# Attention batches turned by VectorE and through memory, and another order of transfers for the turned weights

## The chip, the core and the metric

The kernel runs on one core of a Trainium2 chip. The metric is the device time of one execution in microseconds (us); a kernel's time is the median of its runs. The core has a matrix engine (TensorE, PE in the profile; its weight loads are listed as PEld), a vector engine (VectorE, DVE), a scalar engine (ScalarE, ACT), a general engine (GpSimd, POOL) and SyncE (SP), which computes nothing here and issues nearly all transfers (DMAs). Sixteen DMA engines carry these out. Work happens in on-chip memory of 128 partitions; matmuls write to eight banks of an accumulation memory, each 128 x 512 numbers of float32.

## The reference

The input x has 16 batches of 512 tokens of width 256, all in float32. The block is a "macaron": half a feed-forward part, attention, half a feed-forward part again, with the same feed-forward weights both times.

```python
x = x + 0.5 * _L0_ffn_ref(_layernorm(x), ...)
x = x + _L0_attn_ref(_layernorm(x), Wq, bq, Wkv, bkv, Wo, bo)
x = x + 0.5 * _L0_ffn_ref(_layernorm(x), ...)
```

The feed-forward part is a mixture of 16 slots and 16 experts. The change lies in the attention alone: 16 heads of width 64, queries and keys rotated by position, causal softmax:

```python
q = rope(heads(x @ Wq + bq)); k, v = split(x @ Wkv + bkv); k = rope(heads(k))
scores = einsum('bhqd,bhkd->bhqk', q, k) / sqrt(64)      # masked above the diagonal
out = einsum('bhqk,bhkd->bhqd', softmax(scores), v)
return out @ Wo + bo
```

## The kernel before

All 16 batches stay on chip, with tokens along the partitions (four tiles of 128 tokens). First comes a feed-forward part (to about 430 us), then the attention (to about 1920 us), then the second feed-forward part.

The attention is a loop over 64 units, a unit being one batch and one group of four heads (`units`, L848). It is a pipeline written out by hand (L1101 to L1174): one pass of the loop, called a step here, works on up to four units at once. Step u makes the rotated queries and keys of unit u + 3 (`Rotated`, L886), the scores and exponentials of unit u + 2 (`Weights.scores`, L948; `exps`, L962), scales and turns the weights of unit u + 1 and computes its values (L920), and multiplies the turned weights of unit u with the values (`sums`, L1045) and with Wo (`leave`, L1065). Every engine and every queue takes its instructions in the order in which this loop writes them; the matmuls of a step stand in the order `p_av` (sums), `p_as` (scores of the last token tile), `p_v`, `p_q`, `p_k`, `p_v`, `p_as` (the other tiles), `p_ay` (Wo).

Two things are turned (tokens and another axis exchanged) in this loop.

The first is each batch, once in four units. Queries, keys and values need the normalized batch with its width along the partitions. `enter` (L866) normalizes it with ScalarE into two tiles `h`; `width` (L878) turns it with eight TensorE transposes of 128 x 128 (L883) into two accumulation banks, which ScalarE copies to the tile `ahT` (L884). For the first batch this is done ahead of the loop; for the others in the step in which u + 3 is the first unit of the batch (`fresh`, L1105), the same step whose queries and keys need it. In that step GpSimd also adds the output bias to the batch (`with_bias`, L874). The inverse deviations for a pair of batches come from `spread` (L852, ScalarE) and `scales` (L859, VectorE), one step apart, and from `token_stats` (L193, VectorE), spread over earlier steps.

The second is the softmax weights, in every step. VectorE turns blocks of 32 by 32 (`turn`, L989, instruction at L1001) from the tiles `pr` into the tile `sq`; this exchanges rows and columns within each block, but leaves each block in its group of 32 partitions. `move` (L1018) then brings the blocks to their groups: sixteen transfers, one for each pair of groups (q from, k to), 160 KB each, from `sq` to `prT`. Before the change a source row is one piece of 4 x 320 x 4 = 5120 bytes, and so is a destination row. The transfers run over k outside and q inside. Each of `sq` and `prT` exists once, so a step's turn waits until the transfers of the step before have read `sq`, and the sums (L1054) wait until they have landed.

SyncE issues these sixteen transfers as soon as VectorE has ended the turn, and in the step after a batch's last unit two stores of the finished batch (L1078). The feed-forward parts move their own turned weights through memory in a like way (`Squares`, L518): a store of 512 KB to memory (`leave`, L534) and four loads of 128 KB back (`onto`, L538).

Of the kernel before, what the change touches and what calls it, by code (L numbers as in the profile page):

```python
# [9 lines left out]
F32 = mybir.dt.float32  # L10
# [5 lines left out]
P = 128  # L16
NB, S, D = 16, 512, 256
NT = S // P
NC = D // P
GB = 4  # L20
PB = 2
# [13 lines left out]
HG = 4  # L35
NHG = AH // HG
SQ = 32
NSQ = P // SQ
# [9 lines left out]
def macaron_kernel(ctx: ExitStack, tc: tile.TileContext, a: dict, out: bass.AP):  # L48
# [795 lines left out]
    def attention(qp, wq, wk, wv, wo, cos, sin, row):  # L844
# [2 lines left out]
        ap = None  # L847
        units = [(b, hg) for b in range(NB) for hg in range(NHG)]  # L848
        nu = len(units)
        hTs, hs, qs, ks, vs, oTs, prTs, stds = {}, {}, {}, {}, {}, {}, {}, {}  # L850

        def spread(g):  # L852

            n = PB * NT
            std = small.tile([P, n], F32, tag="std8", name=f"std_g{g}")
            nc.scalar.activation(std, mvs[g][:, :, 1], AF.Sqrt, bias=eps)
            return std

        def scales(g, std):  # L859

            n = PB * NT
            rstds[g] = small.tile([P, n], F32, tag=f"rstd{g}", name=f"rstd{g}", bufs=1)
            nc.vector.reciprocal(rstds[g], std)
            pair_shift(g)

        def enter(b):  # L866

            hs[b] = [qp.tile([P, 2, D], F32, tag=f"rope{2 + k}", name=f"h{b}_{k}") for k in range(2)]
            for t in range(NT):
                i = (b % PB) * NT + t  # L870
                nc.scalar.activation(hs[b][t // 2][:, t % 2, :], xs[b][:, t, :], AF.Identity,
                                     bias=shifts[b // PB][:, i:i + 1], scale=rstds[b // PB][:, i:i + 1])

        def with_bias(b):  # L874
            for t in range(NT):
                nc.gpsimd.tensor_tensor(xs[b][:, t, :], xs[b][:, t, :], row, ALU.add)

        def width(b):  # L878
            hTs[b] = qp.tile([P, NC, S], F32, tag="hT", name=f"ahT{b}", bufs=2)
            for c in range(NC):  # L880
                pt = ps(f"p_ahT{b}_{c}")
                for t in range(NT):
                    nc.tensor.transpose(pt[:, t * P:(t + 1) * P], hs[b][t // 2][:, t % 2, c * P:(c + 1) * P], ident)  # L883
                nc.scalar.copy(hTs[b][:, c, :], pt)  # L884

        class Rotated:  # L886

# [2 lines left out]
            def __init__(self, u, nm, w, r):  # L890
                self.b, self.hg = units[u]
                self.nm, self.w, self.r, self.m = nm, w, r, {}
# [39 lines left out]
        class Weights:  # L932
# [56 lines left out]
            def turn(self, which, heads, of, src, dst):  # L989

                if heads[0] == 0 and which == 0 and len(of) == 2:
                    self.sq = ap.tile([P, NSQ, HG, blocks * SQ], F32, tag="sq", name=f"sq{self.nm}")
                pr = self.pr[which]

                def view(x, at, dims):
                    return bass.AP(x.tensor, x.offset + at, [list(x.ap[0])] + [[s, n] for s, n in dims if n > 1])
                j, nh = heads
                step = (7, 3)[which] * P  # L1000
                nc.vector.transpose(  # L1001
                    view(self.sq, j * blocks * SQ + dst[0] * SQ,
                         [(blocks * SQ, nh)] + [(s * SQ, n) for s, (_, n) in zip(dst[1:], of)]
                         + [(HG * blocks * SQ, NSQ), (1, SQ)]),
                    view(pr, j * step + src * P,
                         [(step, nh)] + [(s * P, n) for s, n in of] + [(SQ, NSQ), (1, SQ)]))

# [10 lines left out]
            def move(self):  # L1018


                prT = prTs[self.u] = ap.tile([P, NSQ, HG, blocks * SQ], F32, tag="prT", name=f"prT{self.nm}")
                for k in range(NSQ):
                    for q in range(NSQ):
                        nc.sync.dma_start(prT[k * SQ:(k + 1) * SQ, q, :, :], self.sq[q * SQ:(q + 1) * SQ, k, :, :])

            def turn_at_once(self):

# [37 lines left out]
        def leave(u, t0):  # L1065
            b, hg = units[u]
            py = ps(f"p_ay{b}_{hg}_{t0}")
            for t in range(2):
                for pair in range(HG // 2):
                    nc.tensor.matmul(py[:, t * D:(t + 1) * D], oTs[u][:, pair, (t0 + t) * P:(t0 + t + 1) * P],  # L1070
                                     wo[:, hg * (HG // 2) + pair, :],
                                     start=(pair == 0), stop=(pair == HG // 2 - 1))

            def added():
                xt = xs[b][:, t0:t0 + 2, :]
                nc.vector.tensor_tensor(xt, py.rearrange("p (t d) -> p t d", t=2), xt, ALU.add)
                if hg == NHG - 1:
                    nc.sync.dma_start(xout[b][:, t0:t0 + 2, :], xt)  # L1078
            return added
# [15 lines left out]
        ap = yield [lambda: width(0)] + queries_keys(0)  # L1095
        ws = {}
        seen = 2 * NHG
        with tc.manual_schedule(engines={mybir.EngineType.DVE, mybir.EngineType.Activation,
                                         mybir.EngineType.Pool, mybir.EngineType.SP}):
            gone = []  # L1100
            for u in range(-2, nu):  # L1101
                new = ws[u + 2] = Weights(u + 2) if u + 2 < nu else None
                qk = queries_keys(u + 3)
                old = ws.get(u + 1)
                fresh = u + 3 < nu and units[u + 3][1] == 0  # L1105
                if fresh:
                    enter(units[u + 3][0])
                if u + 2 == nu:
                    old.scaled((1, 0))
                    values(u + 1, 0)  # L1110
                    values(u + 1, 2)
                if u >= 0:
                    sums(u, 0)
                    sums(u, 1)
                if old and u + 2 == nu:
                    old.turn_at_once()
                elif old:
                    old.turn_most(0)
                    old.scaled((1, 0), slice(0, HG // 2))
                    old.turn_most(1)  # L1120
                    old.scaled((1, 0), slice(HG // 2, HG))
                    old.turn_most(2)
                    old.turn_most(3)
                    old.turn_corner()
                    old.turn_rest()
                    old.move()
                for one in gone:
                    one()
                if fresh:
                    with_bias(units[u + 3][0])  # L1130
                if u + 4 in stds:
                    scales((u + 4) // (PB * NHG), stds.pop(u + 4))
                if fresh:
                    width(units[u + 3][0])
                if new:
                    new.scores((3,))
                    new.exps((3,))

                for at in range(seen, min(u + 13, NB * NHG)):
                    token_stats(*divmod(at, NHG))  # L1140
                seen = max(seen, u + 13)
                if u >= NHG + 1:
                    token_stats(*divmod(u - NHG - 1, NHG))
                if new:
                    new.scaled((3,))
                if 0 <= u + 1 < nu - 1:
                    values(u + 1, 0)
                for one in qk:
                    one()
                if 0 <= u + 1 < nu - 1:  # L1150
                    values(u + 1, 2)
                if 0 <= u + 5 < nu and (u + 5) % (PB * NHG) == 0:
                    stds[u + 5] = spread((u + 5) // (PB * NHG))
                if new:
                    new.scores((2,))
                    new.scores((1, 0))
                    new.exps((2,))
                    new.exps((1, 0), lambda: new.scaled((2,)))

                if u == nu - NHG:  # L1160
                    for g in range(NB // PB - 1):
                        pair_rstd(g)
                if u == nu - 1:
                    for g in range(PB):
                        entered[g] = xs[g]
                        for t in range(NT):
                            i = (g % PB) * NT + t
                            nc.vector.tensor_scalar(xs[g][:, t, :], xs[g][:, t, :], mvs[g // PB][:, i, 0:1],
                                                    rstds[g // PB][:, i:i + 1], ALU.subtract, ALU.mult)
                gone = [leave(u, 0), leave(u, 2)] if u >= 0 else []  # L1170
                if u >= nu - 2:
                    for one in gone:
                        one()
                    gone = []  # L1174
            token_stats(NB - 2, NT - 1)
# [55 lines left out]
```

## Time and profile before

| What | us |
|---|---|
| median of 3 runs (2329.22 to 2330.73) | 2330.49 |
| the profiled execution, its own time | 2332.58 |
| its span in the trace | 2330.9 |
| L883, eight transposes of a batch: time that they hold TensorE in a step | 1.02 |
| L884, one of two evictions of a turned batch, mean | 0.588 |
| L1001, one block turn of 128 x 512, 128 x 768, 128 x 1024, mean | 0.669, 0.950, 1.202 |
| L1024, sixteen transfers of turned weights: issue on SyncE | 10.6 |

How to read it: the profile is one execution. Its span is the time from the first to the last instruction; the execution's own time is 1.7 us longer. Engine names are as above; "SPq" is SyncE's queue of transfers, L12 is line 12 of the kernel. A group's line gives the busy time, the mean length of one instruction and the idle time before it with what ended it. The DMA share is the mean busy share of the 16 DMA engines.

### The profile page before, as it was taken

What the parts mean: (1) busy time and instruction counts of PE and PEld (TensorE: products, weight loads), DVE (VectorE), ACT (ScalarE), POOL (GpSimd) and SP (SyncE); (2) the same over time, 40 slices, a digit from 0 to 9 for tenths busy, and PEclk for the clock granted to TensorE, in tenths of its full rate; (3) what the DMA queues carried; (4) which work ended last, traced back from release to release, by engine and by line L of the source; (5) the groups of instructions that cost most, each with busy time, mean ns of one, the idle gap of its engine ahead of it and who ended that gap; (6) DMA issues with size and microseconds to landing.
All of it is one profiled execution on the core that took longest, in us unless ns stands there. A gap on an engine that the chain in (4) does not pass through costs nothing. (4 is left out here: it accounts for less than half of the span.)

```text
span 2330.9 us, 42260 instructions
## 1 busy us (share of the span) xinstructions
PE 2285.0 (98%) x14496; PEld 1453.5 (62%) x14496; DVE 1754.1 (75%) x4658; ACT 1123.7 (48%) x3046; POOL 1061.9 (46%) x1692
## 2 busy tenths in 40 slices
PE   7999999999999999999999999999999999999999
PEld 5665588465656565565656565655656566664588
DVE  6742397888888888898888888888888874442387
ACT  4743243455455545554645545554555454542233
POOL 2210054565555565655656555556565541210043
PEclk9999999999999999999999999999999999999999
DMA  6839851345555464645455555546464543839834
GB/s 223 252 124 406 321 137 46 85 97 129 107 119 126 103 134 93 142 103 129 107 123 113 126 111 116 129 100 137 91 140 105 127 110 96 241 115 405 329 115 140
DMA packets 159710, 346.77 MB, mean 149 GB/s; under 512 B 38980, under 2 KB 98952, under 8 KB 151304
## 3 DMA queue, kind: packets, MB, share of 16 engines
q1 hardware_dynamic: 158636, 343.27, 55.4%
q8 instruction: 115, 1.88, 0.4%
q14 instruction: 99, 0.81, 0.1%
q10 hardware_dynamic: 860, 0.81, 0.1%
HBM read 148.95 MB, written 29.88 MB: 77 GB/s over the span
## 5 line engine op out<-in xcount | busy, mean ns | idle before, releaser
L986 POOL TENSOR_SCALAR pr<-pr,ars 128x512 f32<-128x512 f32 (+3 forms) x1024 | 522.1, 532 | 631.5 <-DVE ars L983 631.5
L978 ACT ACTIVATE pr<-pr,amn 128x512 f32<-128x512 f32 (+3 forms) x1024 | 560.5, 549 | 268.4 <-DVE amn L974 268.2
L974 DVE CUSTOM_DVE_ANT_0 pr<-p_as,causal 128x512 f32<-128x512 f32 (+3 forms) x1024 | 433.9, 484 | 96.6 <-PE p_as L956 96.6
L1001 DVE STREAM_TRANSPOSE sq<-pr 128x768 f32<-128x768 f32 x441 | 379.0, 906 | 0.2 <-issue 0.2
L956 PE MATMUL p_as<-k,q 32*128 32x128 f32 (+3 forms) x4096 | 325.3, 445 | 7.1 <-DVE k L904 3.4
L1054 PE MATMUL p_av<-prT,v 128*64 128x512 f32 (+3 forms) x2048 | 292.1, 438 | 1.9 <-DVE amn L974 1.9
L956 PEld LDWEIGHTS p_as<-k,q 32*128 32x128 f32 x4096 | 192.4, 186 | 107.4 <-issue 49.6
L920 PEld LDWEIGHTS p_v<-wv,ahT 128*128 128x128 f32 x1024 | 189.4, 190 | 97.4 <-issue 75.6
L920 PE MATMUL p_v<-wv,ahT 128*128 128x256 f32 x1024 | 248.1, 385 | 0.0
L923 ACT COPY v<-p_v 128x512 f32<-128x512 f32 x128 | 73.3, 574 | 353.1 <-PE p_v L920 353.1
L1070 PE MATMUL p_ay<-wo,aoT 128*128 128x256 f32 x1024 | 240.5, 388 | 0.2 <-ACT aoT L1061 0.2
L1054 PEld LDWEIGHTS p_av<-prT,v 128*64 128x64 f32 x2048 | 138.1, 138 | 161.7 <-issue 136.5
L898 PE MATMUL p_k<-ahT,wk 128*128 128x512 f32 x512 | 230.6, 592 | 0.4 <-DVE amn L974 0.4
L898 PE MATMUL p_q<-ahT,wq 128*128 128x512 f32 x512 | 230.5, 593 | 0.2 <-ACT ahT L884 0.2
L1070 PEld LDWEIGHTS p_ay<-wo,aoT 128*128 128x128 f32 x1024 | 190.8, 191 | 32.0 <-ACT aoT L1061 0.6
L978 ACT ACTIVATION_READ_ACCUMULATOR pr<-pr,amn 128x1 f32 x1024 | 191.7, 187 | 0.0
L898 PEld LDWEIGHTS p_k<-ahT,wk 128*128 128x128 f32 x512 | 97.2, 190 | 122.7 <-issue 110.5
L898 PEld LDWEIGHTS p_q<-ahT,wq 128*128 128x128 f32 x512 | 97.1, 190 | 95.8 <-issue 85.4
L717 POOL TENSOR_TENSOR kbd<-kT,own 128x256 f32<-128x256 f32 x32 | 19.7, 619 | 267.4 <-DVE kT L680 235.5
L1061 ACT ACTIVATE aoT<-p_av,bcol 128x512 f32<-128x512 f32 x128 | 87.4, 684 | 108.9 <-PE p_av L1054 108.9
L770 PE MATMUL p_cy<-vw,catT 128*128 128x256 f32 x512 | 120.8, 379 | 0.0
L548 PE MATMUL p_ds<-hT,qk 128*128 128x512 f32 x256 | 118.3, 606 | 2.3 <-ACT hT L241 2.3
(167 smaller groups left out, 3252.0 us busy)
## 6 DMA issues: line engine op xcount, KB each, us to landing
prT<-sq SPq DMA_DIRECT2D x1008, 160.0 KB
w<-in_e_W_dram SPq DMA_DIRECT2D x64, 1024.0 KB
w<-in_e_Wg_dram SPq DMA_DIRECT2D x32, 1024.0 KB
out_dram<-x SPq DMA_DIRECT2D x64, 256.0 KB
awaya<-sqa SPq DMA_DIRECT2D x25, 512.0 KB
atT<-awaya SPq DMA_DIRECT2D x100, 128.0 KB
xl<-in_attn_x_dram SPq DMA_DIRECT2D x16, 512.0 KB
xl<-out_dram SPq DMA_DIRECT2D x16, 512.0 KB
```

The costliest lines, as they stand in the source:

```text
L548: nc.tensor.matmul(psc, qk[:, k, c * P:(c + 1) * P], hT[:, k, :], start=(k == 0), stop=(k == NC - 1))
L770: nc.tensor.matmul(py[:, t * D:(t + 1) * D], atT[:, c, t * P:(t + 1) * P], vws[b][:, c, :], start=(c == 0), stop=(c == NC - 1))
L898: nc.tensor.matmul(pq, self.w[:, k, at:at + P], hTs[self.b][:, k, :], start=(k == 0), stop=(k == NC - 1))
L920: nc.tensor.matmul(pv[:, t * 256:(t + 1) * 256], hTs[b][:, k, (t0 + t) * P:(t0 + t + 1) * P], wv[:, k, hg * HG * DQ:(hg + 1) * HG * DQ], s ...
L956: nc.tensor.matmul(banks[j][:, at:at + w], q[n][j * 32:(j + 1) * 32, i * P:(i + 1) * P], k[n][j * 32:(j + 1) * 32, :w], start=(n == 0), st ...
L974: nc.vector.tensor_tensor_reduce(out=self.at(i, j), in0=banks[j][:, at:at + w], in1=causal[:, S - w:], scale=-1.0 / math.sqrt(DQ), scalar= ...
L978: nc.scalar.activation(self.at(i, j), self.at(i, j), AF.Exp, bias=self.mn[:, i, j:j + 1], scale=-1.0, accum_out=self.rs[:, i, j:j + 1])
L986: nc.gpsimd.tensor_scalar(self.at(i, j), self.at(i, j), self.rs[:, i, j:j + 1], 1.0, ALU.mult, ALU.mult)
L1001: nc.vector.transpose(view(self.sq, j * blocks * SQ + dst[0] * SQ, [(blocks * SQ, nh)] + [(s * SQ, n) for s, (_, n) in zip(dst[1:], of)] + ...
L1054: nc.tensor.matmul(po[j * DQ:(j + 1) * DQ, :].rearrange("d (a f) -> d a f", a=NSQ)[:, :, t * SQ:], vs[u][:, t, head * DQ:(head + 1) * DQ], ...
L1061: nc.scalar.activation(oTs[u][:, pair, :].rearrange("d (i a y) -> d a i y", i=NT, a=NSQ), po.rearrange("d (a i y) -> d a i y", i=NT, a=NSQ ...
L1070: nc.tensor.matmul(py[:, t * D:(t + 1) * D], oTs[u][:, pair, (t0 + t) * P:(t0 + t + 1) * P], wo[:, hg * (HG // 2) + pair, :], start=(pair ...
```

## The change

A batch (but for the first) is no longer turned by TensorE. A new class `Trip` lets VectorE turn its blocks of 32 by 32 with two instructions, straight into the tile `ahT`; SyncE stores this tile to memory in one transfer of 512 KB (`leave`, 4096 bytes a partition), and loads it back with sixteen transfers of 32 KB, one for each pair of groups of 32 partitions, in pieces of 128 bytes at the destination (`land`).

```diff
+        class Trip:
+            def __init__(self, b):
+                self.b = b
+                hTs[b] = qp.tile([P, NC, S], F32, tag="hT", name=f"ahT{b}", bufs=2)
+                dst = hTs[b].rearrange("p c s -> p (c s)").rearrange("p (k c t x) -> p t c k x", k=NSQ, c=NC, t=NT)
+                for i, h in enumerate(hs[b]):
+                    nc.vector.transpose(dst[:, 2 * i:2 * i + 2],
+                                        h.rearrange("p t (c k y) -> p t c k y", c=NC, k=NSQ))
+
+            def leave(self):
+                self.mem = away.tile([P, NC * S], F32, tag="away", name=f"away{self.b}")
+                nc.sync.dma_start(self.mem, hTs[self.b].rearrange("p c s -> p (c s)"))
+
+            def land(self):
+                n = NC * NT
+                for k in range(NSQ):
+                    for a in range(NSQ):
+                        nc.sync.dma_start(
+                            hTs[self.b][k * SQ:(k + 1) * SQ].rearrange("y c s -> y (c s)").rearrange(
+                                "y (n a x) -> a y n x", n=n, a=NSQ)[a],
+                            self.mem[a * SQ:(a + 1) * SQ, k * n * SQ:(k + 1) * n * SQ].rearrange(
+                                "y (n x) -> y n x", n=n))
```

The batch enters a step earlier than before: `enter`, `with_bias` and the turn stand in the step in which u + 4 is the batch's first unit; `land` stands in the next step, near its beginning, ahead of that step's sixteen transfers of weights. `spread`, `scales` and `token_stats` move a step earlier as well.

```diff
-                fresh = u + 3 < nu and units[u + 3][1] == 0
+                fresh = units[u + 4][0] if 0 < u + 4 < nu and units[u + 4][1] == 0 else None
                 if fresh:
-                    enter(units[u + 3][0])
+                    enter(fresh)
+                if u + 3 in trips:
+                    trips.pop(u + 3).land()
...
                 if fresh:
-                    with_bias(units[u + 3][0])
-                if u + 4 in stds:
-                    scales((u + 4) // (PB * NHG), stds.pop(u + 4))
-                if fresh:
-                    width(units[u + 3][0])
+                    with_bias(fresh)
+                    trips[u + 4] = Trip(fresh)
+                    trips[u + 4].leave()
+                if u + 5 in stds:
+                    scales((u + 5) // (PB * NHG), stds.pop(u + 5))
...
-                for at in range(seen, min(u + 13, NB * NHG)):
+                for at in range(seen, min(u + 14, NB * NHG)):
...
-                if 0 <= u + 5 < nu and (u + 5) % (PB * NHG) == 0:
-                    stds[u + 5] = spread((u + 5) // (PB * NHG))
+                if 0 < u + 6 < nu and (u + 6) % (PB * NHG) == 0:
+                    stds[u + 6] = spread((u + 6) // (PB * NHG))
```

The tile `sq` of the turned weights gets its heads ahead of the partition groups, so that a source row of a transfer is four pieces of 1280 bytes; a destination row is contiguous as before. The sixteen transfers go in diagonal order: four in a row have four different sources and four different destinations.

```diff
-                    self.sq = ap.tile([P, NSQ, HG, blocks * SQ], F32, tag="sq", name=f"sq{self.nm}")
+                    self.sq = ap.tile([P, HG, NSQ, blocks * SQ], F32, tag="sq", name=f"sq{self.nm}")
...
-                for k in range(NSQ):
-                    for q in range(NSQ):
-                        nc.sync.dma_start(prT[k * SQ:(k + 1) * SQ, q, :, :], self.sq[q * SQ:(q + 1) * SQ, k, :, :])
+                for n in range(NSQ):
+                    for k in range(NSQ):
+                        q = (k + n) % NSQ
+                        nc.sync.dma_start(prT[k * SQ:(k + 1) * SQ, q, :, :], self.sq[q * SQ:(q + 1) * SQ, :, k, :])
```

The strides that VectorE writes with at L1001 change to match.

More of the change, by code (lines that the diff above doesn't have):

```diff
@@ L849, in attention @@
         nu = len(units)
-        hTs, hs, qs, ks, vs, oTs, prTs, stds = {}, {}, {}, {}, {}, {}, {}, {}
+        hTs, hs, qs, ks, vs, oTs, prTs, stds, trips = {}, {}, {}, {}, {}, {}, {}, {}, {}
         def spread(g):
@@ L1001, in turn @@
                 nc.vector.transpose(
-                    view(self.sq, j * blocks * SQ + dst[0] * SQ,
-                         [(blocks * SQ, nh)] + [(s * SQ, n) for s, (_, n) in zip(dst[1:], of)]
-                         + [(HG * blocks * SQ, NSQ), (1, SQ)]),
+                    view(self.sq, j * NSQ * blocks * SQ + dst[0] * SQ,
+                         [(NSQ * blocks * SQ, nh)] + [(s * SQ, n) for s, (_, n) in zip(dst[1:], of)]
+                         + [(blocks * SQ, NSQ), (1, SQ)]),
                     view(pr, j * step + src * P,
@@ L1097, in attention @@
         seen = 2 * NHG
-        with tc.manual_schedule(engines={mybir.EngineType.DVE, mybir.EngineType.Activation,
-                                         mybir.EngineType.Pool, mybir.EngineType.SP}):
+        with tc.tile_pool(name="awayh", bufs=2, space=bass.MemoryType.DRAM) as away, \
+                tc.manual_schedule(engines={mybir.EngineType.DVE, mybir.EngineType.Activation,
+                                            mybir.EngineType.Pool, mybir.EngineType.SP}):
             gone = []
@@ L1137, in attention @@
                     new.exps((3,))
-                for at in range(seen, min(u + 13, NB * NHG)):
+                for at in range(seen, min(u + 14, NB * NHG)):
                     token_stats(*divmod(at, NHG))
-                seen = max(seen, u + 13)
+                seen = max(seen, u + 14)
                 if u >= NHG + 1:
```

## The prediction

> **What bounds the kernel now.** I read the page first: part 1 for the busy shares, part 5 for the groups of the edited lines.
>
> ```profile
> span 2330.9 us, 42260 instructions
> PE 2285.0 (98%) x14496; PEld 1453.5 (62%) x14496; DVE 1754.1 (75%) x4658; ACT 1123.7 (48%) x3046; POOL 1061.9 (46%) x1692
> ```
>
> TensorE (PE) is busy 98% of the span. A busy PE could hide waits, so the timeline of PE over two steps of the attention loop comes next (a step is one pass of L1101; columns: start, length, engine, line, operation).
>
> ```profile
> 1018.64 4.53 PE L1054 MATMUL p_av<-prT,v 128*64 128x512 f32 x32
> ...
> 1026.86 3.60 PE L898 MATMUL p_q<-ahT,wq 128*128 128x512 f32 x8
> ...
> 1042.01 4.53 PE L1054 MATMUL p_av<-prT,v 128*64 128x512 f32 x32
> 1046.47 1.09 PE L883 MATMUL p_ahT<-ident,h 128*128 128x128 f32 x8
> 1047.49 2.00 PE L956 MATMUL p_as<-k,q 32*128 32x512 f32 x16
> ```
>
> A plain step lasts 1042.01 - 1018.64 = 23.37 us, with one group of matmuls starting as the last ends. A step that turns a new batch holds eight transposes besides, and they hold PE for 1047.49 - 1046.47 = 1.02 us. PE sets the pace, so what leaves PE shortens the end, as long as nothing makes PE wait.
>
> The third view is the queue of SyncE (SP), which issues every transfer of this stage, in program order, and the fourth the DMA share in stretches of 1 us (last two columns: share of the 16 engines, GB/s).
>
> ```profile
> 1024.70 10.60 SPq L1024 DMA_DIRECT2D prT<-sq  x16
> 1035.58 1.18 SPq L1078 DMA_DIRECT2D out_dram<-x  x2
> 1048.08 10.88 SPq L1024 DMA_DIRECT2D prT<-sq  x16
> ```
>
> ```profile
> 1038.00:1039.00 1.00, 1.00 (x19) 0.83 (x14) 1.00 (x5) 1.00 (x5) 0.00 (x0) 1.00 1.02 279
> 1039.00:1040.00 1.00, 1.00 (x7) 0.87 (x6) 1.00 (x9) 1.00 (x4) 0.00 (x0) 1.00 0.71 250
> 1040.00:1041.00 1.00, 1.00 (x6) 0.90 (x5) 0.97 (x10) 1.00 (x6) 0.44 (x1) 1.00 0.05 17
> ```
>
> The sixteen transfers of turned weights (2.62 MB) are issued from 6.06 to 16.66 us after the step's start; with the two stores of the finished batch behind them the engines run dry at about 1040.8, 22.1 us after it. Nobody waits: PE wants the weights at 1042.01.
>
> **The change, part by part.** Write T for the step that now turns the new batch (a step earlier than before; but for the first, the one with the stores) and L for the next one, which lands it and uses it first; times are from the step's start.
>
> *Removed.* In 15 steps (the first batch is still turned by PE ahead of the loop) eight transposes: 15 x 1.02 = 15.3 us off PE. Two evictions each on ScalarE (ACT) go too; ACT is at 48%, so I count nothing.
>
> *VectorE.* Two block transposes of 512 elements a row; the same kind stands in the rows grouped by shape at 669 ns, so 1.34 us in each T, ahead of the subtractions of the mask (L974).
>
> ```profile
> L1001 DVE STREAM_TRANSPOSE sq<-pr 128x512 f32<-128x512 f32 x100 | 66.9, 669 | 0.0
> ```
>
> What hides it is VectorE's own idle time in the same step: 0.38 and 0.19 us in the rotations, and this before the second group of scores:
>
> ```profile
> 1037.14 0.56 DVE L974 CUSTOM_DVE_ANT_0 pr<-p_as,causal 128x384 f32<-128x384 f32 x1 [1.45 <-PE p_as L956]
> ```
>
> Together 2.02 us against 1.34. I cost it at nothing; without that cover, up to 15 x 1.34 = 20 us. The new strides of the weights' turn (L1001) keep its element count; its three forms (669, 950, 1202 ns for 512, 768, 1024) go by elements alone: nothing.
>
> *Earlier by a step.* Normalization, bias and statistics of a batch keep their counts and lengths. A bias costs POOL 4 x 0.73 us, but POOL idles over 7 us a step for sums (L983). Nothing, with 5 us either way as the bound: seven steps around the square roots of the statistics run 0.6 us long today and move along.
>
> *The way through memory.* This is the step that decides. In T, SP issues the 16 weight transfers, the two stores, then the new store of the batch ("leave", 512 KB). In L it issues 16 loads ("land"), and only then that step's 16 weight transfers. The quiet stage at 128 us shows the same trip for the dispatch weights, a store and then four loads:
>
> ```profile
> 128.43 0.34 SPq L534 DMA_DIRECT2D awaya<-sqa  x1
> 131.10 1.73 SPq L538 DMA_DIRECT2D atT<-awaya  x4
> ```
>
> The store is done, and waited out, 2.67 us after its issue, 1.28 of it bytes (64.0% of 16 engines in 129 to 131). In T it lies behind the stores: 22.1 + 1.28 + about 0.5 for its end to be seen = T + 23.9, which is L + 0.5. The loads' own price has a near row, the sixteen loads of query weights, also in pieces of 128 bytes:
>
> ```profile
> 284.11 9.93 SPq L834 DMA_DIRECT2D wq<-in_attn_Wq_dram  x16
> ```
>
> ```profile
> DMA packets 16906, 2.17 MB, mean 107 GB/s; under 512 B 16896, under 2 KB 16896, under 8 KB 16903
> q1 hardware_dynamic: 16903, 2.13, 67.1%
> ```
>
> (285.1 to 305.3 us.) A piece takes 0.671 x 16 x 20.2 / 16903 = 12.8 ns, so the 4096 of a batch are 3.3 us of 16 engines; the issue is slower: 0.62 us for 512 pieces, 0.43 for 128 of 1 KB (atT above). I take 0.50 for 256, so 8 us, and 1.5 to 2 us until the last has landed. Landing: L + 0.5 + 9.7 = L + 10.2. PE wants the batch at p_q, L + 8.22 (1026.86 - 1018.64). **With weight transfers as slow as now PE waits 2.0 us in each L**, more than the 1.02 it saved.
>
> *Pieces of 1280 bytes, diagonal.* No row shows this form. Between 1025.8 and 1039.5 the engines are 98.4% busy at 225 GB/s, stores included; the weights alone make about 213, or 12.3 us. Yet wider transfers move much more in the same engine time: 315 GB/s for the store at 129 us. Slices of 0.34 us inside that very stretch reach 419. So engines are not at their limit; something in how 32 partitions are read and written is. Rotating the target group may relieve it. Upper bound of the gain: the bytes keep up with SP's issue and end 1.5 us after it; the batch's store then waits for nobody, is done at T + 18.5 + 2.67 = T + 21.2 or L - 2.2, and the batch lands at L + 7.5: no wait. Lower bound, a loss: pieces of 128 bytes at 12.8 ns and of 4096 at 160 give 8 ns for each piece and 37 ns a KB; four of 1280 then cost 24 ns more than one of 5120, 0.8 us on each engine a step, and the wait is 2.8 us. I take 246 GB/s, the best full microsecond of the nearest row (loads into 32 partitions, 133 to 134 us): 2.62 MB in 10.7 us, 1.6 sooner, so a wait of 0.4 us.
>
> The Trainium skill speaks against this: "SBUF — State Buffer", section "Can I just issue two DMAs to hit both halves?", says that transfers on different halves of the partitions serialize, with 6% gained. By it the weights would take 11.6 us, the wait would be 1.3 us and the time about 2335. The 419 GB/s slices say that more can be had.
>
> *L's other load.* The weight transfers of L start when land is issued, at L + 5.8 to 8.5 instead of 6.06, and end up to 2.5 us later. Their cover: PE needs them at 23.37 and VectorE overwrites their source from 22.8; they end at 19.4 in a step without stores (1014.7 for the step at 995.28). 3.4 us of room, so nothing; past it, each us costs 15 us.
>
> *Sum.* 15 x (1.02 - 0.4) = 9.3 us. The profiled execution took 2332.58 us (span 2330.9 plus 1.7 around it), so 2323.3; it lay 2.1 above the median of the runs, 2330.49, against which I forecast 2321.
>
> **Rivals.** All gains and losses under 0.2% (4.7 us) count as no change, about what a measurement of this kernel can tell.
>
> - *A, the batch lands in time or nearly* (wait 0 to 0.7 us): 2315 to 2326, the forecast 2321. For it: the double rate in slices, and a cover of 22 us. Against: it needs 1.3 us from transfers whose new form no row shows.
> - *B, it lands about 1 us late* (0.7 to 1.3): 2326 to 2335, the gain eaten by the new wait. Speed-up 0.7 to 1.3 us.
> - *C, slower: PE waits for the batch at p_q in L.* Place: L898 with ahT, 15 times. From a wait of 1.02 us it loses. Unchanged transfers: 15 x (2.0 - 1.02) = +15, 2345; dearer pieces: 15 x (2.8 - 1.02) = +27, 2357. For it: SP's queue as it stands. Against: only if the order of the pieces brings nothing.
> - *D, VectorE's 1.34 us a batch isn't absorbed*, and PE waits for banks that L974 or L904 free late: up to 20 - 15.3 = +5, 2335. Against: the 1.45 us idle row.
> - *The change doesn't do what it says*: if the transfers were still cut at 5120 bytes, only their order would count; this lies inside B and C.
>
> **How the numbers follow.** A 0.50, B 0.14, C 0.30, D 0.06. Faster 0.50, same 0.14, slower 0.36 (C and D). The likeliest alone spans 2315 to 2326. The range runs from 2313 (all 15.3 us and 2 of the 5 from the moved statistics) to 2350, which takes in C up to a wait of 2.3 us and leaves out dearer pieces, some 0.13.
>
> **What would show it.** L883 in the loop gone: 8 records left of 128, steps that were 24.39 now 23.37. The packets: some 129,000 of 1280 bytes in place of 32,256 of 5120, and 61,440 more under 512 bytes. In the step after a turn, p_q either starts 8.2 us after p_av (A) or later, with a wait for a DMA named (C). The 16 weight transfers' bytes should end at 17 to 18.5 us of a plain step rather than 19.4. In T, the idle row before L974 shrinks from 1.45; if it is gone and PE waits there, D. I am wrong most of all if land is issued at 0.62 us, as wq was (2 us later), or if the transfers speed up so far that the wait never was near.

## The result and the profile after

| | kernel before | changed kernel |
|---|---|---|
| median of 6 runs each, us | 2329.56 (2328.36 to 2330.73) | 2337.16 (2336.01 to 2344.36) |
| the profiled execution, its own time, us | 2332.58 | 2336.01 |
| attention loop in the two traces, start of its first step to start of its last, us | 1489.7 | 1494.6 |

The ratio is 1.0034 (95% interval 1.0024 to 1.0044): slower by 0.34%. The forecast was 2321, faster; the case that came true is the place and sign of rival C, at a smaller price. The two traces differ by 3.4 us and the medians by 7.6, because the profiled execution of before lies above all six of its runs, and that of after is the fastest of its six. So the traces show what happens; the runs say how much.

The page of the changed kernel: TensorE is 10 us less busy than before, and yet the span is longer.

```profile
span 2334.3 us, 42312 instructions
PE 2274.5 (97%) x14376; PEld 1441.7 (62%) x14376; DVE 1771.3 (76%) x4688; ACT 1109.5 (48%) x3016; POOL 1064.6 (46%) x1692
```

The timeline of PE in the changed kernel, the step that turns a batch (T, from 1018.96) and the next, which lands it (L, from 1042.42):

```profile
1018.96 4.53 PE L1082 MATMUL p_av<-prT,v 128*64 128x512 f32 x32
...
1042.42 4.53 PE L1082 MATMUL p_av<-prT,v 128*64 128x512 f32 x32
1046.88 2.00 PE L983 MATMUL p_as<-k,q 32*128 32x512 f32 x16
1048.81 1.99 PE L947 MATMUL p_v<-wv,ahT 128*128 128x256 f32 x8
1051.48 3.67 PE L925 MATMUL p_q<-ahT,wq 128*128 128x512 f32 x8 [0.68 <-ACT pr L1005]
```

The transposes are gone and T lasts 23.46 us. But in L the queries start 9.06 us after the step's start instead of 8.22. Over all L steps but the first (where T holds no stores) this delay is 0.47 to 2.07 us, 1.28 in the mean, 17.9 in the sum: more than the 15.3 that left. (T and L are the prediction's two steps: T turns and stores a batch, L is the next one and loads it.) The queue of SP in the same two steps says why:

```profile
1025.02 10.33 SPq L1052 DMA_DIRECT2D prT<-sq  x16
1035.47 1.05 SPq L1106 DMA_DIRECT2D out_dram<-x  x2
1036.62 0.44 SPq L901 DMA_DIRECT2D away<-ahT  x1
1041.98 7.75 SPq L907 DMA_DIRECT2D ahT<-away  x16
1049.84 11.28 SPq L1052 DMA_DIRECT2D prT<-sq  x16
```

The batch's store is issued 17.7 us into T, behind the 16 weight transfers and the two stores. SP sees it done 5.4 us later, T + 23.0; in the quiet stage a store of the same size took 2.67. Then 16 loads in 7.75 us, 0.48 each; the last is issued at 1049.73, and 1.75 us later the queries start. The DMA share in T shows the queue of bytes in front of the batch (last two columns: share of the 16 engines, GB/s):

```profile
1034.00:1036.00 2.00, 2.00 (x13) 1.47 (x15) 1.84 (x3) 0.03 (x1) 2.00 (x2) 1.00 1.13 212
1038.00:1039.00 1.00, 1.00 (x25) 0.88 (x18) 1.00 (x7) 0.94 (x3) 0.88 (x1) 1.00 1.10 216
1039.00:1040.00 1.00, 1.00 (x6) 0.87 (x6) 1.00 (x7) 1.00 (x5) 0.00 (x0) 1.00 1.11 393
1040.00:1041.00 1.00, 1.00 (x6) 0.90 (x5) 0.97 (x7) 1.00 (x5) 0.13 (x1) 1.00 1.06 429
1041.00:1042.00 1.00, 1.00 (x6) 0.87 (x6) 1.00 (x9) 1.00 (x6) 1.00 (x3) 1.00 0.34 123
```

Up to 1038.2 it is the weights that move (212 GB/s with the engines counted as full), then their last bytes and the two stores, up to 1040.2. The batch itself moves from 1039.8 to 1041.5 (start and end of packets in the trace).

One reading needs care. In its list of waits the profile puts most of the wait at the queries down to ScalarE:

```profile
PEld p_q L925 <- ACT pr L1005: 20.5, 14, 2.3
...
PE p_q L925 <- ACT pr L1005: 11.4, 11, 1.8
PE p_q L925 <- DMA ahT<-away: 4.3, 3, 1.9
```

So "the queries wait for the landing" is so far one theory, and "they wait for ScalarE or VectorE, which the change loads otherwise" a rival.

### The profile page after: what moved, and what is told of

It is laid out like the page before. It is cut to its first block, busy times and chain, and to the rows that moved or that the text cites. A ratio compares the mean times of both kernels' runs of the same rounds, so it can differ in the third digit from the quotient of the medians.

```text
span 2334.3 us, 42312 instructions
## 1 busy us (share of the span) xinstructions
PE 2274.5 (97%) x14376; PEld 1441.7 (62%) x14376; DVE 1771.3 (76%) x4688; ACT 1109.5 (48%) x3016; POOL 1064.6 (46%) x1692
## 5 line engine op out<-in xcount | busy, mean ns | idle before, releaser
L1001 DVE CUSTOM_DVE_ANT_0 pr<-p_as,causal 128x512 f32<-128x512 f32 (+3 forms) x1024 | 433.4, 483 | 72.9 <-PE p_as L983 72.8
```

What stands on the lines that cost most here:

```text
L1001: nc.vector.tensor_tensor_reduce(out=self.at(i, j), in0=banks[j][:, at:at + w], in1=causal[:, S - w:], scale=-1.0 / math.sqrt(DQ), scalar= ...
```

## The experiments

**Theory 1**: the batch lands late, since its store stands behind the weights and stores in SP's queue and its loads need 7.7 us of issue; the weights' new form is no faster. **Rivals**: the weights' new form costs the time; the queries are held by another engine; the loads are slow wherever the store stands.

### One part alone

`w_only`: the kernel before with the new form of the weights (rows of 4 x 1280 bytes, diagonal order), nothing else.

> The kernel before with the weights' part alone: rows of four pieces of 1280 bytes, diagonal order; batches still turned by TensorE. Theory 1 (the change lost because the batch lands late; the new form of the weight transfers brings no speed): bytes of the sixteen transfers end 19 to 20.5 us after a step's start as in both traces, nobody waits for them, time 2329 to 2331, no change. Rival (the new form itself costs the time, by dearer pieces or by VectorE's new strides at the turn): slower by 3 us or more, and the turn's mean of 906 ns or the bytes' end moves up.

Measured: 2330.52 us, ratio 0.9999 (0.9990 to 1.0009) to the kernel before, which was run again beside each group of experiments; each ratio here is to those runs. In plain steps the weights' bytes end 20.2 us after the start, before 20.1 (from the packets of the traces). The strides cost VectorE nothing: 669, 950 and 1202 ns, as before. The weights' part alone changes nothing in the time.

`trip_only`: the changed kernel with the old rows and the old order, that is the batches' way through memory alone.

> The change without the weights' part: 5120-byte rows and the old order, batches through memory. Theory 1: the batch is as late as in the changed kernel, TensorE waits about 1.3 us at p_q in 14 steps, time 2334 to 2340. If the new form of the transfers did help the landing a little, up to 2347 (a wait of 2.0 us). Rival (the weights' part is what costs): 2314 to 2320.

Measured: 2335.04 us, ratio 1.0020 (1.0010 to 1.0029); waits in L of 1.17 us in the mean (1.28 in the changed kernel). Most of the loss sits in this part: 4.0 us against the kernel before, where the changed kernel lost 7.6. The intervals of the two ratios overlap, so whether the weights' form adds to it isn't settled.

### Taking the landing away

`no_land`: the changed kernel without its sixteen loads.

```diff
-                    trips.pop(u + 3).land()
+                    trips.pop(u + 3)
```

> The changed kernel without the sixteen loads: the batch stays turned in blocks only, so queries, keys and values of batches 1 to 15 are made from wrongly placed numbers; all other work is there. Theory 1: no wait at p_q at all, steps of 23.4 us throughout: 15.3 us less on TensorE than the kernel before, 2314 to 2318. Rival (something other than the landing holds p_q, as ScalarE's exponentials, which the trace names for part of the waits): p_q still starts 9 us or later in the landing steps, 2330 or more.

Measured: 2316.26 us, ratio 0.9941 (0.9926 to 0.9956). PE in the landing step of this kernel, from 1033.58:

```profile
1033.58 4.53 PE L1082 MATMUL p_av<-prT,v 128*64 128x512 f32 x32
1038.04 2.00 PE L983 MATMUL p_as<-k,q 32*128 32x512 f32 x16
1039.97 2.00 PE L947 MATMUL p_v<-wv,ahT 128*128 128x256 f32 x8
1041.80 3.60 PE L925 MATMUL p_q<-ahT,wq 128*128 128x512 f32 x8
```

The queries start at 8.22 us in every step of the loop but the first. ScalarE and VectorE have the same work as in the changed kernel, so it wasn't they that held PE. This is also the floor of the idea: 14.8 us below the kernel before, run beside it (2331.04), nearly all of the 15.3.

### Moving the store in the queue

`leave_first`: the batch is turned and stored ahead of the finished batch's additions and stores.

```diff
+                if fresh:
+                    trips[u + 4] = Trip(fresh)
+                    trips[u + 4].leave()
                 for one in gone:
                     one()
                 if fresh:
                     with_bias(fresh)
-                    trips[u + 4] = Trip(fresh)
-                    trips[u + 4].leave()
```

> The changed kernel with one block moved: the batch is turned and its store issued ahead of the additions and stores of the finished batch, so on SyncE's queue it stands before the two stores instead of behind them. Theory 1: the store is issued about 1 us earlier and waits for 1.7 us less of bytes, so the batch lands 2 to 3 us earlier and the wait at p_q of 1.3 us goes: 14 x 1.3 = 18 us less than the changed kernel, 2317 to 2322, faster than the kernel before by 8 to 13. Rival (the step is long for VectorE's or ScalarE's load, not for the landing): within 3 us of the changed kernel, or slower, since the additions come 1.3 us later.

Measured: 2322.86 us, ratio 0.9966 (0.9955 to 0.9978), 0.9 us above what was expected. The loads are issued 1.3 us earlier than in the changed kernel (T + 21.9 against 23.2, means of 14 steps), not 2 to 3, so a wait of 0.4 us is left in the mean. The store still stands behind the sixteen weight transfers:

```profile
1022.50 10.37 SPq L1052 DMA_DIRECT2D prT<-sq  x16
1032.98 0.53 SPq L901 DMA_DIRECT2D away<-ahT  x1
1033.61 1.67 SPq L1106 DMA_DIRECT2D out_dram<-x  x2
1038.18 8.08 SPq L907 DMA_DIRECT2D ahT<-away  x16
```

`leave_act`: the store alone goes to ScalarE's queue.

```diff
-                nc.sync.dma_start(self.mem, hTs[self.b].rearrange("p c s -> p (c s)"))
+                nc.scalar.dma_start(self.mem, hTs[self.b].rearrange("p c s -> p (c s)"))
```

> The changed kernel with the batch's store issued from ScalarE's queue instead of SyncE's. Theory 1 (what makes the batch late is that its store stands behind the sixteen weight transfers and two stores): the store leaves as soon as VectorE has turned the batch, some 9 us into the step instead of 17.7, is done well before SyncE reaches the loads, and these are issued in the same step right behind the stores of the finished batch, at 17 to 25 us; the batch lands about 3 us into the next step, nobody waits, and that step's weight transfers start on time again: 2314 to 2319, as without the loads. Rival (the loads themselves take too long, wherever the store stands, or a store among the weight transfers makes these late): 2322 or more.

Measured: 2318.16 us, ratio 0.9946 (0.9931 to 0.9961). The queue of SP in its steps T (from 1011.42) and L (from 1034.87):

```profile
1017.48 11.70 SPq L1052 DMA_DIRECT2D prT<-sq  x16
1029.29 1.07 SPq L1106 DMA_DIRECT2D out_dram<-x  x2
1030.45 9.64 SPq L907 DMA_DIRECT2D ahT<-away  x16
1040.84 11.31 SPq L1052 DMA_DIRECT2D prT<-sq  x16
```

```profile
1019.82 0.33 ACTq L901 DMA_DIRECT2D away<-ahT  x1
```

The store is issued 8.4 us into T, when SP has issued three or four of the sixteen weight transfers (14 steps), instead of behind all of them. Its bytes move amid the weights' and are through 12.2 us into T (mean), not 22.7. The loads follow right behind the stores, the batch lands 6.1 us into L (expected 3: the loads take 9.6 us to issue beside the weights' bytes), and L's weights start at 5.97. No wait is left in any step. PE in L:

```profile
1034.87 4.53 PE L1082 MATMUL p_av<-prT,v 128*64 128x512 f32 x32
...
1043.09 3.17 PE L925 MATMUL p_q<-ahT,wq 128*128 128x512 f32 x7
```

### Fewer loads

`land4`: the pieces of 128 bytes go to the store's side; four stores and four loads with contiguous rows replace one and sixteen.

```diff
             def leave(self):
-                self.mem = away.tile([P, NC * S], F32, tag="away", name=f"away{self.b}")
-                nc.sync.dma_start(self.mem, hTs[self.b].rearrange("p c s -> p (c s)"))
+                self.mem = away.tile([SQ, NSQ * NC * NT, NSQ, SQ], F32, tag="away", name=f"away{self.b}")
+                for a in range(NSQ):
+                    nc.sync.dma_start(
+                        self.mem[:, :, a, :],
+                        hTs[self.b][a * SQ:(a + 1) * SQ].rearrange("y c s -> y (c s)").rearrange("y (m x) -> y m x", x=SQ))
...
+                for k in range(NSQ):
+                    nc.sync.dma_start(
+                        hTs[self.b][k * SQ:(k + 1) * SQ].rearrange("y c s -> y (c s)"),
+                        self.mem[:, k * n:(k + 1) * n].rearrange("y n a x -> y (n a x)"))
```

> The changed kernel with the pieces of 128 bytes moved to the store: four stores of 32 partitions that write the memory in the batch's final order, and four loads of 128 KB with contiguous rows of 4096 bytes in place of sixteen; same place in SyncE's queue. If the sixteen issues of the loads (7.7 us of the queue) are the larger part of the lateness: four stores cost 1.5 us more of issue and some 2 us more of bytes than one, four loads 5.8 us less, so the batch lands 2 to 3 us earlier; the wait of 1.3 us goes or nearly goes: 2316 to 2324. If pieces of 128 bytes are dearer when written to memory (over 30 ns each, against 13 when read), the store takes 5 us longer and nothing is won: 2334 or more.

Measured: 2317.25 us, ratio 0.9948 (0.9931 to 0.9965), no wait left. SP in T (from 1010.95) and L (from 1034.40):

```profile
1028.75 5.26 SPq L902 DMA_DIRECT2D away<-ahT  x4
1036.64 1.73 SPq L909 DMA_DIRECT2D ahT<-away  x4
1040.38 10.52 SPq L1052 DMA_DIRECT2D prT<-sq  x16
```

The store side is dearer than I had said: its four issues take 5.3 us rather than 2, and the third of the four alone takes 2.5 (median of 15). That it has to wait for bytes ahead of it is likely, but no run tests it. The loads begin 2.4 us later than in the changed kernel. But these take 1.7 us of issue instead of 7.7, and the batch has landed 5.7 us into L instead of 8.9 (means). A piece written to memory took 13.8 ns, hardly more than the 12.7 of one read.

### Order and pieces apart

`w_diag5120` is the kernel before with the diagonal order alone, `w_rows1280` with the short pieces alone. The diff is that of the first; the second has the new tile `sq` and its strides, with the old loops.

```diff
-                for k in range(NSQ):
-                    for q in range(NSQ):
-                        nc.sync.dma_start(prT[k * SQ:(k + 1) * SQ, q, :, :], self.sq[q * SQ:(q + 1) * SQ, k, :, :])
+                for n in range(NSQ):
+                    for k in range(NSQ):
+                        q = (k + n) % NSQ
+                        nc.sync.dma_start(prT[k * SQ:(k + 1) * SQ, q, :, :], self.sq[q * SQ:(q + 1) * SQ, k, :, :])
```

> The kernel before with the diagonal order alone, rows of one piece of 5120 bytes. The weights' part as a whole brought no speed; either neither half does anything (bytes end 19.5 to 20.5 us after a step's start, as before), or order and pieces cancel: then the bytes end 1 us or more earlier here and later with the pieces alone. Time 2328 to 2333 in any case, since nobody waits for these bytes.

> The kernel before with rows of four pieces of 1280 bytes in the old order. If neither half does anything: bytes end at 19.5 to 20.5 us. If order and pieces cancel: 1 us or more later (the 0.8 us of dearer pieces that the prediction allowed for). Time 2328 to 2333 in any case.

Measured: 2329.59 and 2329.92 us, one run each. The queue's line (packets, MB, share of 16 engines' span) before, of the order alone, of the pieces alone, and of both (`w_only`):

```profile
q1 hardware_dynamic: 158636, 343.27, 55.4%
```

```profile
q1 hardware_dynamic: 158636, 343.27, 52.9%
```

```profile
q1 hardware_dynamic: 255404, 343.27, 60.5%
```

```profile
q1 hardware_dynamic: 255404, 343.27, 58.3%
```

The same bytes are counted with less engine time in the diagonal order and with more in short pieces. A packet of 5120 bytes took 372 ns before and 344 in diagonal order; four of 1280 took 429 in the old order and 404 in the diagonal one. In plain steps the bytes end at 20.1 us before, 19.2 with the order, 20.9 with the pieces, 20.2 with both. So both halves work, in opposite directions. The moves of 0.9 and 0.8 us fall just short of the "1 us or more" that I had set as the sign, but 19.2 and 20.9 also lie outside the 19.5 to 20.5 of "neither half does anything", and the packets agree in direction. They cancel in the moment at which the bytes end, not in engine time: with both, the share is 58.3% against 55.4.

### The prediction's own arithmetic, tried out

`trip_diag5120`: the changed kernel with the order kept and the rows of one piece restored.

> The changed kernel with rows of one piece of 5120 bytes, its diagonal order kept. The looks at the halves showed the order ending the weights' bytes 0.9 us earlier and the pieces ending them 0.8 us later. Theory 1 (each us by which the weights' bytes end later lands the batch a us later and costs 14 us): the batch lands some 0.9 us earlier than with the old order and rows (2335) and than in the changed kernel (2337), so 11 to 13 us less: 2322 to 2326. Rival (the weights' transfers don't set when the batch's store is done): 2333 to 2338.

Measured: 2321.28 us, ratio 0.9964 (0.9951 to 0.9978), 13.8 below `trip_only` (13 by the ratios) and 0.7 under what was expected. The mean wait in L falls from 1.17 to 0.41 us, and the loads are issued 0.9 us earlier (T + 22.25 against 23.11). Less than a microsecond of DMA time in a step thus decides whether the change wins or loses.

`best`: `land4` with this form of the weights.

> Four stores and four loads for a batch, as in the run that had these, and the weights in rows of 5120 bytes in diagonal order. Theory 1: no wait for the batch, nothing left to gain from faster weights: 2315 to 2319, as with the four stores alone and as without the loads; faster than the kernel before by 11 to 15 us. If a late batch still costs something there: up to 3 us less than the 2317 of that run.

Measured: 2315.55 us (2313.43 to 2318.03), ratio 0.9936 (0.9923 to 0.9948). It beats both kernels: 14.4 us below the kernel before, run beside it, at the floor that `no_land` showed. Whether it beats `land4` (2317.25, not run beside it) is not settled: neither has a wait left, and the two spreads overlap.

## Why the prediction failed

- **What left TensorE: right.** 1.02 us a batch, 15 times; `no_land` is 14.8 us faster than the kernel before.
- **VectorE: right.** The two turns take 680 ns each (669 predicted). T stays within 0.1 us of a plain step (0.4 in one of 14), and the idle row ahead of the second scores shrank but is there:

```profile
1037.45 0.56 DVE L1001 CUSTOM_DVE_ANT_0 pr<-p_as,causal 128x384 f32<-128x384 f32 x1 [0.25 <-PE p_as L983]
```

  Rival D is out: `leave_act` and `land4` have the same two turns and reach the floor.
- **The way through memory: right in its mechanism and place, a little too dear.** Store done at T + 23.0 in the step shown, 23.2 in the mean (predicted 23.9 without faster weights), 7.75 us of issue for the loads (8), 1.75 until the queries start (1.7): a wait of 1.28 us in the mean of 14 steps (not 15: the first L has none) where "as slow as now" gave 2.0. The 0.7 us between them is one term, the 22.1 at which T's stores are through: in the changed kernel, and in `trip_only` with the old weights, they are through at 21.4. The rest of the sum (1.28 + 0.5 for the store, 8 + 1.7 for the loads) came as written. Why T's stores end sooner wasn't tested. The pieces of 128 bytes cost 12.7 ns, as the row had it.
- **The step that failed: "I take 246 GB/s, ... 10.7 us, 1.6 sooner, so a wait of 0.4 us."** The weights came no sooner: 20.2 us against 20.1. I had set the relief by the order against the price of the pieces as two ends of one range and taken a value near the good end. They are two independent terms, and both came: the order gave 0.9 us and the pieces took 0.8. That the latter is the size of my lower bound is partly luck: four pieces took 57 ns more than one of 5120 bytes, not 24, so 1.8 us on each engine, of which 0.8 shows at the end of the bytes. With both put in, the wait would have been about 2.0 us by my other terms and the forecast 2345, rival C. The choice of row was bad too: 133 to 134 us shows loads from memory, which read no partition. And I had read the end of today's bytes too early: "19.4" is 20.5 in that step's packets, 20.1 in the mean.
- **The page weighed.** The Trainium skill, "SBUF — State Buffer", section "Can I just issue two DMAs to hit both halves?", gives 6% for transfers on different halves. The order alone brought 344 against 372 ns, 8%; no run has the page's own case, two transfers at once on opposite halves. The rule was the better guide than the fast slices, which I had read as room that an order could reach. The view counts a packet's bytes in the slice in which it starts; a slice of 0.34 us is shorter than a packet (0.37), and the one of 419 GB/s stands next to one of 105. That the page's sum, 2335, lies near the measured 2337 is luck: its 0.7 us sooner came, but from T's earlier stores and not from the weights.
- **What stays open**: 4.2 us, the gap between the difference of the medians (7.6) and that of the traces (3.4). In the traces the loop is 4.9 us longer: waits of 17.9 less the 15.3 that left, 1.0 in the steps T, 1.0 in the steps L beyond the waits, 0.2 at its two ends; and it starts 1.5 us earlier. The waits range from 0.5 to 2.1 us within one trace, so runs with longer ones are likely, but one trace can't show it. Why the diagonal order helps, and only by 8%, wasn't tested either.

## What to carry to other kernels

In this kernel a transfer placed last in a queue paid for the bytes ahead of it: a store of 512 KB took 2.7 us on an idle queue, and 5.4 (mean) with some 0.8 MB of others' bytes still to move. Where a round trip through memory replaces work on the bounding engine, write its deadline down in the step's own clock, and look for another queue (one word of code here) or fewer issues before making the transfers ahead of it faster. And where a change alters two things in the same transfers, price them as two terms with signs of their own; a change that leaves the time as it was may be two effects that cancel.

## What the runs showed of the hardware

- Between two groups of 32 partitions sixteen transfers ran at 212 GB/s with the DMA engines counted as full (share 1.13, 1034 to 1036 us of the changed kernel's trace); a few microseconds later stores from 128 partitions moved 393 and 429 GB/s at shares of 1.11 and 1.06. In these rows a full share says nothing of the rate.
- A store issued from ScalarE's queue, when three or four of SP's sixteen transfers had been issued, was through at 12.2 us of the step; placed behind all of them in SP's queue it was through at 22.7. While its 128 packets moved, 126 packets of the weights started (mean of 14 steps, 74 to 244). The Trainium skill, "DMA: Bandwidth & Descriptors", section "Queues, rings and completion order", says that each DMA engine takes turns between the queues that have work; the run agrees. That the store passed many transfers issued before it isn't shown: these had nearly all begun to move when its first bytes did.
- In the list of waits, the queries' matmuls and weight loads (PE and PEld), which waited for a DMA, stand under ScalarE 25 times out of 28; only the run without the loads settled it.
